# Attention scores as sixteen products on 32x32 tiles of the array

## The chip, the core and the metric

The kernel runs on one core of one Trainium2 chip. The metric is the device time of one execution in microseconds (us). Before the change it was 3142.55 us, the median of 3 runs (3142.08 to 3144.96).

## What is computed

Two attention layers on an image batch x of shape (4, 256, 64, 64), all in float32, with 8 heads of 32 channels. Cut to what matters here:

```python
# layer 0: keys and values at half resolution (1024 keys for 4096 queries)
q = einsum('oc,bchw->bohw', Wq, gn(x));  k, v = conv2x2(gn(x), Wk), conv2x2(gn(x), Wv)
attn = softmax((q.k + q.pos) * 32**-0.5);  x = x + v.attn
# layer 1: four areas of 1024 positions, each attends to itself
q, k, v = conv1x1(gn(x), w_qkv)
out = softmax(q.k * 32**-0.5).v + dwconv7(v, w_pe);  x = x + conv1x1(out, w_proj)
```

Both layers have the same attention: for each head, 4096 queries against 1024 keys, with a product over 32 channels for the scores and one over the keys for the result.

## The kernel before

The work is cut into units of 512 queries and 4 heads (16 units for an image and layer, 128 in all), and a unit into 8 key blocks of 128 keys. A key block of a unit is a "step"; there are 1024. The loop at the end of `direct_path` takes a step and a half in each of its 683 phases. In a phase, `scores(f)` computes one step over all 512 queries (`full`) and one half of another step, over 256 queries (`half`), for 4 heads each: eight products.

A score product (`score_product`, line 360) has the keys of one head as its weights, 32 rows (channels) by 128 columns (keys), and the head's queries as the moving operand, 32 rows by 512 or 256 columns. Head h lies in rows 32h to 32h+31 of the array, a "row group", so that the products of four heads run side by side in the four row groups. Each covers all 128 columns of the array, and writes 128 partitions of PSUM. The order of a phase is: `half` for heads 1 and 3, `full` for heads 0, 2, 1 and 3, a fence, and `half` for heads 0 and 2.

The three PSUM tiles of a phase (`a`, `b`, `c`, of two banks each, all called `s` in the profile) hold full heads 0 and 2, full heads 1 and 3, and the half step. In `c`, heads 0 and 1 share a bank, as heads 2 and 3 do. Two row groups may not write one bank at the same time, and so TensorE waits, at the fence, until the products of heads 1 and 3 have been counted in the semaphore `in_bank`. Each of these products adds one to it when it is done, and `bank_count` is the number that the fence waits for. What follows the fence in TensorE's queue is also behind it.

ScalarE takes the exponential of `a`, `b` and `c` (lines 401 and 412). In the next phase, `weighted` (line 426) multiplies these with the values: four products of 128 rows by 32 columns, one for each head, side by side in the four "column groups" of the array. VectorE adds up the exponentials (line 436) for the divisors. Between the scores and the `weighted` products of a phase, TensorE may have a side product (projections through `product`, line 164, the convolution on lines 973 and after, or the divisors, line 445), all of them four products of 32 columns side by side. A planner (`plan`, `task`, `side_parts`) chooses them by due times, before the program runs; the instruction order on each engine is written out by it.

Of the kernel before, what the change touches and what calls it, by code (L numbers as in the profile page):

```python
# [15 lines left out]
P = 128  # L16
# [3 lines left out]
NH, HD = 8, 32  # L20
# [39 lines left out]
def direct_path(  # L60
# [19 lines left out]
    V, S, G, T = nc.vector, nc.scalar, nc.gpsimd, nc.tensor  # L80
# [31 lines left out]
    first = [pool.tile([P, CT, CH], FP, tag="p", name=f"first_{c}", bufs=PB) for c in range(PB)]  # L112
    rest_of_first = pool.tile([P, 4, CH], FP, tag="acc", name="first", bufs=2)
    first += [rest_of_first[:, :2, :], rest_of_first[:, 2:, :]]
    for c in range(NCH):
# [27 lines left out]
        out=gmat, in_=gmat, compare_op=ALU.is_ge, fill=0.0, base=0,  # L143
# [3 lines left out]
        out=gmat, in_=gmat, compare_op=ALU.is_ge, fill=0.0, base=7,  # L147
# [18 lines left out]
    def ps_banks(n, name):  # L166
        return psum.tile([P, 2, CH], FP, tag=f"s{n}", name=name, bufs=1)
# [174 lines left out]
    in_bank, bank_count = tc.alloc_semaphore("in_bank"), [0]  # L342

    def acc_of(g):
        if g not in accs:
            accs[g] = pool.tile([P, 4, CH], FP, tag="acc", name="acc", bufs=2)
        return accs[g]

    def pair_of(h):
        return slice(2 * (h % 2), 2 * (h % 2) + 2)  # L350

    def acc_half(g, u):
        return acc_of(g).rearrange("p (l b) (u n) -> p u b l n", l=2, u=2)[:, u]

    def parts_of(f):

        full, half = (3 * f + 1) // 2, (3 * f // 2 + 1, 0) if f % 2 == 0 else (3 * f // 2, 1)
        return (full if full < last else None), (half if half[0] < last else None)

    def score_product(out, s, h, cols):  # L360
        g, j = divmod(s, NKT)
        rows, unit = slice(HD * h, HD * h + HD), units[g]
        return T.matmul(  # L363
            out, lhsT=unit[2]()[rows, unit[0], j * P : (j + 1) * P], rhs=unit[1]()[rows, cols], start=True, stop=True
        )

    def scores(f):

        full, half = parts_of(f)
        a, b, c = [ps_banks(n, "s") for n in ((0, 1, 2) if f % 2 == 0 else (0, 2, 1))]  # L370
        every = slice(0, CH)

        def half_product(h):

            u = half[1]
            return score_product(
                c[:, h // 2, HC * (h % 2) : HC * (h % 2) + HC], half[0], h, slice(HC * u, HC * u + HC)
            )

        if half is not None:  # L380
            for h in (1, 3):
                first = half_product(h).then_inc(in_bank, 1)
                tc.add_to_no_dep_group(f"first_{f}", first.ins)
                tc.no_tile_sem_insts.add(first.ins.name)
                bank_count[0] += 1
        for h in (0, 2, 1, 3):
            score_product((a, b)[h % 2][:, h // 2, :], full, h, every)
        if half is not None:
            fence = T.wait_ge(in_bank, bank_count[0])
            tc.declare_fence(fence.ins, group=f"first_{f}")  # L390
            for h in (0, 2):
                half_product(h)

        def exp_full(n):
            g, j = divmod(full, NKT)
            if j == 0:
                p = acc_of(g)[:, pair_of(n), :]
            else:
                p = pool.tile([P, 2, CH], FP, tag="p", name="p", bufs=PB)
            made_p[full, n] = p  # L400
            S.activation(p, (a, b)[n], AF.Exp, scale=SCALE)  # L401

        def exp_half():
            if half is None:
                return
            (g, j), u = divmod(half[0], NKT), half[1]
            if j == 0:
                p = acc_half(g, u)
            else:
                p = pool.tile([P, 2, CH], FP, tag="p", name="p", bufs=PB).rearrange("p b (l n) -> p b l n", l=2)  # L410
            made_p[half[0], 2 + u] = p
            S.activation(p, c.rearrange("p b (l n) -> p b l n", l=2), AF.Exp, scale=SCALE)  # L412

        return [lambda: exp_full(0), lambda: exp_full(1), exp_half]
# [663 lines left out]
    f = step = 0  # L1078
    before = []
    while f < PHASES or before or plan or side or quick or norms_left or to_add or to_divide:  # L1080
        now[0], phase[0] = step, f
        exps = scores(f) if f < PHASES else [lambda: None] * 3
        mine = []
        if f < PHASES:
# [641 lines left out]
```

## Time and profile before

| | us |
|---|---|
| median of 3 runs | 3142.55 |
| the profiled execution | 3136.07 |
| its span, first to last instruction | 3134.3 |
| TensorE (PE) matmuls, busy | 3059.4 (98%) |
| TensorE weight loads (PEld), busy | 1413.7 (45%) |
| VectorE (DVE) busy | 2516.0 (80%) |
| ScalarE (ACT) busy | 2456.4 (78%) |
| GpSimd (POOL) busy | 486.3 (16%) |

The granted clock of TensorE was 0.997 of full speed. The profiled execution is one run of the program under the hardware profiler. PE is the matmul, PEld the weight load that goes ahead of it. Matmuls are pipelined and the profiler models their ends, so a busy PE says that work is in flight, not that the array is full. A row of a group gives the line in the kernel, the engine and operation, the names of the tiles (output, then inputs), the shape, the count, then the busy time in us and the mean duration in ns, then the idle time of the engine ahead of them and what ended it. For a matmul, `32*128 32x512` is a weight block of 32 rows by 128 columns and a moving operand of 32 rows by 512 columns. A row of the timeline gives the start and length in us of a merged stretch of like instructions, and how many they are.

### The profile page before, as it was taken

The numbers are of one execution on the slowest core, as the hardware profiler recorded it, in microseconds if no ns is written. First come the engines' busy times: TensorE is split into PE (matmuls) and PEld (weight loads), VectorE is DVE, ScalarE is ACT, GpSimd is POOL, SyncE is SP. The second block draws the span as 40 slices with busy tenths as digits, with TensorE's granted clock in tenths as the row PEclk, the third lists the DMA queues.
The fourth block names the chain that finished last, engine by engine and source line by source line (L and its number), as shares of the span: only waits on it lengthen the run. The fifth ranks groups of instructions, "written<-read, shape, count | busy, mean of one in ns | idle before, by whom it ended". The sixth has DMA issues, their size and how long they took to land.

```text
span 3134.3 us, 87972 instructions
## 1 busy us (share of the span) xinstructions
PE 3059.4 (98%) x36218; PEld 1413.7 (45%) x36218; DVE 2516.0 (80%) x2719; ACT 2456.4 (78%) x2988; POOL 486.3 (16%) x923
## 2 busy tenths in 40 slices
PE   7999999999999999999999999999999999999997
PEld 4344444444455554444444444444444444444442
DVE  3788898878887777878778888788787888888887
ACT  2888878888788878878877777788887777778774
POOL 0111111111121111111111111111111111111111
PEclk9999999999999999999999999999999999999999
DMA  5243444556455646567777666664566556633212
GB/s 187 50 99 79 119 96 92 124 107 146 123 158 140 169 139 160 120 163 180 199 188 183 163 159 176 159 170 123 126 137 155 143 153 176 166 101 85 65 43 69
DMA packets 648236, 422.29 MB, mean 135 GB/s; under 512 B 411772, under 2 KB 556636, under 8 KB 647832
## 3 DMA queue, kind: packets, MB, share of 16 engines
q1 hardware_dynamic: 619384, 380.11, 47.7%
q0 software_dynamic: 28448, 36.48, 4.5%
q8 instruction: 292, 4.78, 0.7%
q14 instruction: 112, 0.92, 0.1%
HBM read 318.32 MB, written 98.09 MB: 133 GB/s over the span
## 4 chain that ended last, share of the span: by engine, by line
PE 46%; issue 4%; DMA 2%; ACT 1%; DVE 1%; POOL 1%; SPq 0%; ACTq 0%; DVEq 0%; POOLq 0%
PE s L363 16%; PE av L426 13%; PE q1ps L164 4%; PE ops L164 4%; PE k1ps L164 3%; PE conv_ps L973 2%; PE den L445 2%; PE vals_ps L164 1%; DMA recs<-few 1%; DVE acc L436 1%; ACT p L401 1%; POOL rb L474 0%; SPq L732 0%; DMA rb<-recs 0%; DMA cv<-conv 0%
## 5 line engine op out<-in xcount | busy, mean ns | idle before, releaser
L436 DVE TENSOR_TENSOR acc<-acc,p 128x1024 f32<-128x1024 f32 x1790 | 2113.2, 1218 | 457.9 <-ACT p L401 180.7
L401 ACT ACTIVATE p<-s 128x1024 f32<-128x1024 f32 x1194 | 1160.4, 1025 | 458.2 <-PE s L363 445.4
L412 ACT ACTIVATE p<-s 128x1024 f32<-128x1024 f32 x598 | 619.9, 1037 | 2.7 <-DVE acc L436 1.7
L363 PE MATMUL s<-q,k_A 32*128 32x256 f32 (+1 forms) x5464 | 559.8, 510 | 9.1 <-ACT p L401 6.2
L363 PE MATMUL s<-q,k_B 32*128 32x512 f32 (+1 forms) x5456 | 551.3, 509 | 2.6 <-ACT p L401 2.1
L363 PEld LDWEIGHTS s<-q,k_B 32*128 32x128 f32 x5456 | 342.8, 183 | 281.2 <-issue 55.1
L363 PEld LDWEIGHTS s<-q,k_A 32*128 32x128 f32 x5464 | 338.0, 183 | 291.7 <-ACT p L401 66.4
L426 PE MATMUL av<-p,v_A 128*32 128x256 f32 (+1 forms) x4784 | 454.0, 487 | 0.0
L426 PE MATMUL av<-p,v_B 128*32 128x512 f32 (+1 forms) x4776 | 451.2, 487 | 0.0
L474 POOL DMA_DIRECT2D rb<-recs x508 | 252.0, 502 | 510.0 <-DMA recs<-few 426.5
L472 POOL DMA_DIRECT2D recs<-few x127 | 70.1, 552 | 1413.5 <-DVE sums L471 1241.0
L426 PEld LDWEIGHTS av<-p,v_B 128*32 128x32 f32 x4776 | 148.5, 110 | 258.7 <-issue 233.1
L426 PEld LDWEIGHTS av<-p,v_A 128*32 128x32 f32 x4784 | 148.7, 110 | 235.6 <-issue 196.8
L401 ACT ACTIVATE acc<-s 128x1024 f32<-128x1024 f32 x172 | 166.9, 1023 | 78.7 <-PE s L363 78.5
L445 PE MATMUL den<-acc,ones 128*32 128x512 f32 x1024 | 144.6, 606 | 6.8 <-DVE acc L436 3.6
L464 POOL DMA_DIRECT2D few<-rows x127 | 72.3, 569 | 414.1 <-DMA rows<-den_sb 409.7
L164 PE MATMUL ops<-cv,wp_sb 128*32 128x512 f32 x1024 | 125.0, 602 | 5.2 <-DVE cv L744 4.4
L164 PE MATMUL k0ps<-taps,wkv 128*32 128x256 f32 x2048 | 124.9, 386 | 2.5 <-ACT taps L328 2.5
L164 PE MATMUL q1ps<-h,wqkv_sb 128*32 128x512 f32 x1024 | 123.8, 598 | 1.9 <-ACT q L701 1.9
L164 PE MATMUL vals_ps<-hv,wqkv_sb 128*32 128x512 f32 x1024 | 123.8, 598 | 0.2 <-ACT gmean_A L299 0.2
L164 PE MATMUL k1ps<-h,wqkv_sb 128*32 128x512 f32 x1024 | 123.5, 598 | 0.0
L164 PE MATMUL q0ps<-hq,wq_sb 128*32 128x512 f32 x1024 | 122.8, 597 | 0.0
(99 smaller groups left out, 2123.9 us busy)
## 6 DMA issues: line engine op xcount, KB each, us to landing
rows<-vals SPq DMA_DIRECT2D x384, 195.9 KB
rb<-recs POOLq DMA_DIRECT2D x508, 64.0 KB, 2.6
share<-vals SPq DMA_DIRECT2D x128, 195.9 KB
vala<-vout SPq DMA_DIRECT2D x128, 144.0 KB
vals<-vout SPq DMA_DIRECT2D x128, 144.0 KB
vc<-vala SPq DMA_DIRECT2D x64, 288.0 KB
band<-mats SPq DMA_DIRECT2D x96, 176.0 KB
hq<-in_x SPq DMA_DIRECT2D x32, 512.0 KB
```

The source lines that it names most:

```text
L164: T.matmul(out[cols, :], lhsT=lhsT[:, cols], rhs=rhs, start=start, stop=stop)
L363: return T.matmul(out, lhsT=unit[2]()[rows, unit[0], j * P : (j + 1) * P], rhs=unit[1]()[rows, cols], start=True, stop=True)
L401: S.activation(p, (a, b)[n], AF.Exp, scale=SCALE)
L412: S.activation(p, c.rearrange("p b (l n) -> p b l n", l=2), AF.Exp, scale=SCALE)
L426: T.matmul(out, lhsT=v[:, j, unit[0] * P + HD * h : unit[0] * P + HD * h + HD], rhs=rhs, start=(j == 0 and not u), stop=(j == NKT - 1), sk ...
L436: V.tensor_add(to, to, p)
L445: T.matmul(dens[g][HD * h : HD * h + HD, :], lhsT=ones, rhs=p(h), start=(n == 0), stop=(n == len(sets) - 1),)
L464: G.dma_start(few[:, 0, :], rows.rearrange("h (q n) -> (h q) n", n=CH // HD))
L472: G.dma_start(recs.rearrange("h (q n) -> (h q) n", n=CH // HD), few[:, 1, :])
L474: G.dma_start(rb[HD * h : HD * h + HD, :], recs[h : h + 1, :].to_broadcast([HD, CH]))
L973: T.matmul(ps[HD * m : HD * m + HD, (2 * k + i) * size : (2 * k + i + 1) * size].rearrange("p (y x) -> p y x", y=NY), lhsT=band[:, half].r ...
```

## The change

`score_product` issues four products where it issued one: the 128 keys are cut into four blocks of 32, and each block goes with its own 32 columns of weights to its own 32 partitions of the same output. The queries are the same for all four. Four heads give sixteen products on sixteen tiles of 32 rows by 32 columns. Because `score_product` now returns a list, the two half products in front of the fence become eight, each with its own increment of `in_bank`; the fence waits for eight more each phase instead of two. The order of everything else, on all engines, is as before, and no wait is added or taken away.

```diff
     def score_product(out, s, h, cols):
         g, j = divmod(s, NKT)
         rows, unit = slice(HD * h, HD * h + HD), units[g]
-        return T.matmul(
-            out, lhsT=unit[2]()[rows, unit[0], j * P : (j + 1) * P], rhs=unit[1]()[rows, cols], start=True, stop=True
-        )
+        return [
+            T.matmul(
+                out[n : n + HD], lhsT=unit[2]()[rows, unit[0], j * P + n : j * P + n + HD],
+                rhs=unit[1]()[rows, cols], start=True, stop=True,
+            )
+            for n in range(0, P, HD)
+        ]
...
         if half is not None:
             for h in (1, 3):
-                first = half_product(h).then_inc(in_bank, 1)
-                tc.add_to_no_dep_group(f"first_{f}", first.ins)
-                tc.no_tile_sem_insts.add(first.ins.name)
-                bank_count[0] += 1
+                for first in half_product(h):
+                    first.then_inc(in_bank, 1)
+                    tc.add_to_no_dep_group(f"first_{f}", first.ins)
+                    tc.no_tile_sem_insts.add(first.ins.name)
+                    bank_count[0] += 1
```

## The prediction

> **What bounds the kernel now.** I read the page's first section, then the groups with shapes kept apart, the groups of the score tile, a timeline of one phase, and last the trace's own records of single instructions and semaphore updates. The first view is the page:
>
> ```profile
> span 3134.3 us, 87972 instructions
> PE 3059.4 (98%) x36218; PEld 1413.7 (45%) x36218; DVE 2516.0 (80%) x2719; ACT 2456.4 (78%) x2988; POOL 486.3 (16%) x923
> ...
> q8 instruction: 292, 4.78, 0.7%
> ```
>
> (The last line is the queue that fetches instructions: packets, MB, share of the DMA engines.) TensorE has work in flight nearly always, at a granted clock of 0.997; VectorE and ScalarE have a fifth of the time to spare. So a change of TensorE's time per phase shows nearly one to one. There are 683 phases of 3134.3/683 = 4.59 us. The groups, with shapes kept apart:
>
> ```profile
> L363 PE MATMUL s<-q,k_A 32*128 32x512 f32 x2728 | 545.4, 616 | 0.4 <-ACT p L412 0.4
> ...
> L363 PE MATMUL s<-q,k_A 32*128 32x256 f32 x2736 | 451.5, 404 | 8.7 <-ACT p L401 6.2 <-ACT acc L401 1.8 <-ACT q L597 0.7
> ...
> L426 PE MATMUL av<-p,v_B 128*32 128x512 f32 x2392 | 313.0, 593 | 0.0
> ...
> L973 PE MATMUL conv_ps<-rows,band 88*32 88x128 f32 x3072 | 98.2, 276 | 0.2 <-DMA rows<-vals 0.2
> ```
>
> Each fp32 product is two matmuls ("passes"), each with a weight load. The score rows hold 10920 matmuls (5464 + 5456 on the page): 5460 products, eight a phase, four of 512 columns and four of 256 (682 phases have the halves). Next, the score tile's own view, and one phase in the timeline:
>
> ```profile
> L363 PEld LDWEIGHTS s<-q,k_A x5464: 181/184/186, 82.0 to 1597.8; 32*128 32x128 f32 x196
> L363 PE MATMUL s<-q,k_A x5464: 374/478/692, 82.0 to 1598.0; 32*128 32x256 f32 x147, 32*128 32x512 f32 x49
> ```
>
> ```profile
> 1507.82 0.61 PE L426 MATMUL av<-p,v_A 128*32 128x256 f32 x8
> ...
> 1508.36 1.19 PEld L363 LDWEIGHTS s<-q,k_A 32*128 32x128 f32 x16 [0.41 <-ACT vout L901]
> 1508.36 1.59 PE L363 MATMUL s<-q,k_A 32*128 32x256 f32 x16
> ...
> 1509.88 0.16 PEld L164 LDWEIGHTS vals_ps<-hv,wqkv_sb 128*32 128x32 f32 x8 [0.33 <-issue]
> 1509.88 0.64 PE L164 MATMUL vals_ps<-hv,wqkv_sb 128*32 128x512 f32 x4
> ```
>
> ```profile
> 1509.22 0.22 PEld L363 LDWEIGHTS s<-q,k_A 32*128 32x128 f32 x2
> ```
>
> The last line, a narrow window, is the first weight load behind the fence: 0.86 us after the phase's first. The single records, as medians over 679 phases and counted from the phase's first weight load, give this anatomy. Heads 1 and 3 (half) and 0 and 2 (full) start at 0.002 to 0.022 us, 6.7 ns apart. Their first pass lasts 104 ns more than the same shape later (692 against 587, 478 against 374): the exposed load of 128 weight columns. The halves' second pass starts at 0.322 and 0.328, the fulls' at 0.538 and 0.544; heads 1 and 3 (full) run from 0.548; heads 0 and 2 (half) start at 0.978 and 0.984, and the last column has streamed at 1.428. A 512-column pass occupies its tile 0.428 us (the starts of av's passes), a 256-column one 0.215, so a row group needs 2 x (0.428 + 0.215) = 1.286: streaming is the bulk of the 1.428. Before the scores there are 94 ns, after them 89 ns (medians), in which nothing streams.
>
> **The change, part by part.**
>
> *Streaming: nothing.* A 32x32 tile still takes a column of q at the same pace; sixteen tiles read as much per partition as av's four tiles of 128x32 do, and av gets its full pace (0.428 per pass, four at once). No row has 32x32 tiles.
>
> *Weight loads: about nothing.* A load of 32 columns exposed after a switch costs 25 ns (vals' first pass 617 against 592), so 79 ns less than now. But the first wave is now sixteen products, not four. Starts are 6.7 ns apart, which is four instructions, so the sixteenth tile starts at 0.027 + 15 x 0.0067 = 0.128. Today the fourth streams from 0.022 + 0.104 = 0.126. The gain is eaten by the queue.
>
> *The fence: the cost.* The fence on `in_bank` must see heads 1 and 3 done before heads 0 and 2 may write the same banks. Today two increments feed it, afterwards eight. The records put the two updates 42 to 43 ns apart in nearly every phase, though their matmuls start 6 ns apart, and no two of the 4338 updates by TensorE are closer than 42 ns. So I take eight at 42.5 ns. Today: the second passes start at 0.322 and end 0.374 later, the first update comes 0.014 after that (0.710), the second at 0.753, the weight load behind the fence at 0.858: 0.105 after the last update. That is just hidden: heads 0 and 2 are free at 0.97 and 0.98 and need 104 ns of weights. Afterwards:
> head 1's first tile streams from 0.027, its second pass starts at 0.242, the first update comes at 0.242 + 0.374 + 0.014 = 0.630, the eighth at 0.630 + 7 x 0.0425 = 0.928, the first load behind the fence at 1.033. Behind a fence the second product comes 35 ns later (the L973 products after one released at 1542.25 show 35 and then 7 ns each), so the eighth loads at 1.033 + 0.035 + 6 x 0.0067 = 1.108, streams from 1.133, and ends two passes of 0.215 later at 1.563. It could have started at 0.128 + 2 x 0.428 = 0.985. So the scores end 1.563 - 1.428 = 0.135 us later.
>
> What is queued behind: the two halves, then av or a side product, which need the array emptied of the scores' tile shape, so all of it moves by 0.135. ScalarE's third exp waits too, but it has about 1 us to spare in each phase. Some 5% of the phases already stall by 0.4 us or more on other things and may absorb it. Sum: 682 x 0.135 = 92 us, less 5% = 87 us. Against the profiled execution's 3136.07 us that is 3223; the median of the timed runs lies 6.5 us above that execution, so about 3230.
>
> Bounds. If updates of different tiles did not queue, the load behind the fence would come at 0.663 + 0.014 + 0.105 = 0.782, hidden, and the scores would end at 0.985 + 0.43 = 1.415: 682 x -0.013 = -9 us. The nearest row is the pair at 42.5, of different tiles too, so I take that.
>
> The Trainium skill ("TensorE: Matmul & The Clock Gate", The cost: per-tile semaphore tail) also says that increments of tiles serialize, at 26.3 ns each. By that figure the eighth update comes at 0.814, the end is at about 1.449, and the sum is an estimated +14 us; this trace's 42 ns differs, and the measurement decides.
>
> *Instructions.* 16380 more products are 32760 more matmuls and as many weight loads. In a phase the scores issue 128 instead of 32. The burst pace is 6.7 ns for four (214 ns for 128, hidden in 1.28 us of streaming). The longest dense stretch, L973's 64 matmuls with their loads, keeps 13.3 ns per instruction over 128, but streaming binds there, so that is an upper bound. At it, the 32 instructions behind the fence take 0.43 us and the eighth product starts some 0.32 later than above: another 682 x 0.32 = 220 us. I take the burst pace, as the row right behind a fence shows it, and keep the other for the range.
>
> The same page (Wait — 56ns, not 53.3ns?) says that matmul starts are never under 25 ns apart, which speaks against this change: 64 x 25 ns = 1.6 us would not fit the streaming, an estimated 0.32 us a phase or +218 us. This trace's starts on different tiles are 6.7 ns apart, so I do not use it.
>
> The instruction queue carries 65520 x 64 B = 4.2 MB more, some 256 packets of 1.2 us (0.7% of 16 engines' span over 292). The DMA engines are busy 0.77 of a dense stretch at 1500 us, so I cost this at nothing; were each packet waited for, it would be 307 us.
>
> **The rivals.**
>
> *Faster: no emptying between 32x32 and 128x32 tiles.* Both cut the columns in four. If the 94 and 89 ns vanished, 682 x 0.183 = 125 us would go, and with the fence's 92 the time would be about 3110. It decides once the switches shrink by more than 0.135 a phase. For it: products of one shape (vals to av) follow without a gap. Against it: rows still go from 128 to 32, and both directions show a gap today. 8%.
>
> *Hidden fence.* At half the measured spacing, 21 ns, the eighth update comes at 0.630 + 0.149 = 0.779, the load behind the fence at 0.884, the eighth product at 0.98, in time: 3142.55 - 9 = 3133. A few ns more of spacing gives up to 3160. Against it, 42 ns in every phase. 13%.
>
> *Slow issue.* The queue does not hold the 32 instructions behind the fence, or the sixteen tiles of a wave start late: up to 92 + 220, so 3265 to 3455. Nothing in the trace shows more than 16 in a burst. 18%.
>
> *The tiles of a row wait for each other.* A product's second pass stands ahead of the next product in program order. Today the next one overtakes it, but it is always in another row group, or for av in another column group. If tiles sharing a row group queued in order, each product would start a pass after the one before: 4 x 0.643 + 0.43 = 3.0 us against 1.43, +1.57 x 682 = 1070 us, about 4210. 7%. That the change does nothing at all is not open: the instructions are there.
>
> **How the numbers follow.** Forecast 3230 with 54% (3190 to 3265), and the rivals as above. The range 3133 to 3440 takes in the forecast, the hidden fence and nearly all of slow issue, and leaves out the no-emptying and row-queue cases, some 18% with the edges. Within 0.2% (about what a measurement of this kernel can tell from no change) lie 3136 to 3149: 8%, from the hidden fence. Faster: 8% and a few points of the hidden fence, 12%. Slower: 80%.
>
> **What would show it.** Right: x68978 matmuls; eight updates of `in_bank` 42 ns apart; the first weight load behind the fence at about 1.03 us instead of 0.86 while heads 0 and 2 stand idle; first passes 25 ns over the later ones; switches still of 90 ns. Wrong: a load behind the fence before 0.95; starts of sixteen tiles spread over more than 0.15 us; tiles of one row starting 0.2 us apart; a gap that is gone at a switch.

## The result, and the profile after

The changed kernel takes 3378.51 us (median of 4 runs, 3367.82 to 3385.28) against 3142.32 us before (4 runs, 3141.22 to 3144.96): a ratio of 1.0749, with a 95% interval of 1.0735 to 1.0764. The forecast was +88 us, the measured difference is +236 us. The sign was right, and the size was off by a factor of 2.7.

The page's first section, and its row of the queue that fetches instructions:

```profile
span 3366.0 us, 153492 instructions
PE 3299.6 (98%) x68978; PEld 1498.6 (45%) x68978; DVE 2522.3 (75%) x2719; ACT 2467.0 (73%) x2988; POOL 484.6 (14%) x923
...
q8 instruction: 548, 8.98, 1.1%
```

The products are there (68978 matmuls). VectorE and ScalarE do the same work in the same time, and PE is again 98% busy. That share says only that some tile has work in flight. What is lost in this kernel is lost while PE counts as busy. The instruction queue has its 256 more packets. The granted clock was 0.998.

The groups, with shapes kept apart (busy time in us, mean ns of one):

```profile
L364 PE MATMUL s<-q,k_A 32*32 32x512 f32 x10912 | 657.1, 599 | 0.1
L364 PE MATMUL s<-q,k_A 32*32 32x256 f32 x10944 | 496.4, 385 | 6.5 <-issue 2.4 <-ACT p L406 2.0 <-ACT acc L406 1.3
```

There are four times as many matmuls, and each one is shorter than before (599 ns against 616, 385 against 404), because less of a weight load is exposed in front of a first pass. So no single product became slower. The time lies between products. The timeline of one phase (start, length, how many), and, of the weight loads alone, a narrow window in it:

```profile
1505.34 0.61 PE L431 MATMUL av<-acc,v_A 128*32 128x256 f32 x8
1505.89 1.97 PE L364 MATMUL s<-q,k_A 32*32 32x256 f32 x64
1507.78 1.06 PE L450 MATMUL den<-acc,ones 128*32 128x512 f32 x8
```

```profile
1506.56 0.10 PEld L364 LDWEIGHTS s<-q,k_A 32*32 32x32 f32 x1
```

The stretch of score matmuls is 1.97 us long; it was 1.59. The narrow window holds one load, 0.67 us after the phase's first (1505.884). It is not the load behind the fence, but one that the prediction had not put on the path: the second product of full head 1. The same phase cut into stages, for the score tile alone (stage, length, then busy time and count of PE and of PEld, ScalarE, granted clock, DMA share, GB/s), shows its place:

```profile
1505.88:1506.01 0.13, 0.12 (x16) 0.13 (x30) 0.00 (x0) 1.00 1.10 216
1506.01:1506.34 0.33, 0.33 (x24) 0.22 (x29) 0.00 (x0) 1.00 0.99 195
1506.34:1506.55 0.21, 0.21 (x25) 0.10 (x1) 0.00 (x0) 1.00 0.46 104
1506.55:1506.83 0.28, 0.28 (x25) 0.27 (x13) 0.00 (x0) 1.00 0.39 103
```

In the first 0.13 us sixteen products start. In the third row, 0.46 to 0.67 us, one load is made, although the eight tiles of heads 1 and 3 come free between 0.46 and 0.50. Then thirteen loads come in 0.28 us.

The trace's single records (medians over 679 phases, in us from the phase's first score weight load) give the whole order:

| event | before | after |
|---|---|---|
| the first wave starts | 0.002 to 0.022 (4) | 0.002 to 0.120 (16) |
| second pass of heads 1 and 3 (half) | 0.322, 0.328 | 0.242 to 0.288 |
| updates of `in_bank` | 0.710, 0.753 | 0.629, then 42.5 ns apart, to 0.927 |
| full heads 1 and 3: first product starts | 0.548 | 0.458 |
| their others load | (0.555 starts) | 0.674, then 42.5 ns apart; the last starts at 0.932 |
| first and second load behind the fence | 0.858, 0.893 | 1.032, 1.127 |
| halves 0 and 2 end | 1.428 | 1.681 |
| full heads 1 and 3 end | 1.40 | 1.810 |
| gaps in front of and behind the scores | 94, 89 ns | 94, 89 ns |

The last row but two was the end of the scores before, and the last row but one is the end after. The means from trace to time: a phase's score stretch went from 1.472 to 1.831 us (+0.359, less than the median's +0.382), and the mean gaps around it gave back 0.021. The sum, 0.339 x 682 = 231 us, is the difference of the two spans (3366.0 - 3134.3 = 231.7).

The full heads 1 and 3 run late for a reason that the prediction had not asked about. Seven of their eight products load 44 ns or so after one update of `in_bank` each (0.629 and 0.674, and so on at the same pace), although nothing in the kernel makes them wait for that semaphore. This gave the theories that the experiments were to tell apart. In program order a phase has 32 products: 1 to 8 are the halves of heads 1 and 3, 9 to 16 full heads 0 and 2, 17 to 24 full heads 1 and 3, and 25 to 32, behind the fence, the halves of heads 0 and 2.

**Theory W (window).** TensorE holds 64 instructions, which are 16 products of four instructions each (load, matmul, load, matmul). They go out in program order, each when it is complete and its increment is written; only then does a new one come in. The 16 products of the first wave fill it. The 17th (full head 1's first) gets in piece by piece as the first leaves: its load at 0.243, its first pass at 0.458. The 18th waits until the first product of half head 1 is out: 0.242 + 0.374 = 0.616, and its increment at 0.629. The next products get in as the others of heads 1 and 3 leave, and since each of these carries an increment, they leave 42.5 ns apart. The last, head 3's fourth, starts at 0.932, has its second pass at 1.383 and ends 0.428 later: 1.811 (measured 1.810). In the same way the 26th, the second product behind the fence, waits for the 9th, full head 0's first: 0.508 + 0.587 = 1.095 (its load is at 1.127).

**Rivals.** The increments alone make the delay, and without them the 18th product would start when its tile is free, at about 0.5; or TensorE is short of instructions, and the new ones come at a slow pace wherever they stand.

### The profile page after: what moved, and what is told of

The parts are those of the page before. It is cut to its first block, busy times and chain, and to the rows that moved or that the text cites. A ratio compares the mean times of both kernels' runs of the same rounds, so it can differ in the third digit from the quotient of the medians.

```text
span 3366.0 us, 153492 instructions
## 1 busy us (share of the span) xinstructions
PE 3299.6 (98%) x68978; PEld 1498.6 (45%) x68978; DVE 2522.3 (75%) x2719; ACT 2467.0 (73%) x2988; POOL 484.6 (14%) x923
## 5 line engine op out<-in xcount | busy, mean ns | idle before, releaser
L364 PE MATMUL s<-q,k_A 32*32 32x512 f32 (+1 forms) x21856 | 680.0, 492 | 6.5 <-issue 2.4
L364 PE MATMUL s<-q,k_B 32*32 32x512 f32 (+1 forms) x21824 | 675.0, 492 | 0.9 <-issue 0.4
L364 PEld LDWEIGHTS s<-q,k_A 32*32 32x32 f32 x21856 | 377.0, 103 | 310.3 <-ACT p L417 78.8
L364 PEld LDWEIGHTS s<-q,k_B 32*32 32x32 f32 x21824 | 380.0, 103 | 301.7 <-issue 69.4
```

Of the source, the lines that this page charges most:

```text
L364: T.matmul(out[n : n + HD], lhsT=unit[2]()[rows, unit[0], j * P + n : j * P + n + HD], rhs=unit[1]()[rows, cols], start=True, stop=True,)
```

## The experiments

**Two increments in sixteen tiles.** Only the last column block of heads 1 and 3 counts; the sixteen products stay.

```diff
-                for first in half_product(h):
-                    first.then_inc(in_bank, 1)
+                for n, first in enumerate(half_product(h)):
+                    if n == P // HD - 1:
+                        first.then_inc(in_bank, 1)
+                        bank_count[0] += 1
...
-                    bank_count[0] += 1
```

> The changed kernel, but only the last column block of heads 1 and 3 counts into in_bank: two increments a phase instead of eight. Theory W (TensorE holds 64 instructions at once and lets them go in program order, each when its matmul is complete and its increment is written; a product is four instructions, so product k of a phase gets in when product k-17 is out): the increments no longer add 42 ns each, but the second wave (full heads 1 and 3) still waits until the first product is complete at 0.62 us, and the halves of heads 0 and 2 until full head 0 is complete at 1.10. The scores end at 1.68 us in the phase instead of 1.81: 3378.5 - 682 x 0.13 = about 3290. Rival I (the increments alone hold things up): the fence is hidden and the scores end at 1.41 to 1.43: 3133 to 3145. Rival S (TensorE's instructions are supplied too slowly for four times as many): hardly changed, 3340 to 3380.

Measured: 3308.13 us (4 runs), ratio to before 1.0535 (1.0518 to 1.0553). The phase ends at 1.682. Updates come at 0.680 and 0.773, and the first load behind the fence at 0.878. The stages of a phase that starts at 1504.677, columns as above:

```profile
1504.68:1504.81 0.13, 0.13 (x16) 0.13 (x31) 0.00 (x0) 1.00 0.78 167
1504.81:1505.14 0.33, 0.33 (x25) 0.22 (x28) 0.00 (x0) 1.00 0.71 183
1505.14:1505.31 0.17, 0.17 (x25) 0.10 (x1) 0.00 (x0) 1.00 0.74 235
1505.31:1505.48 0.17, 0.17 (x29) 0.15 (x14) 0.00 (x0) 1.00 0.67 188
```

The same hole stands in the third row: one load between 0.46 and 0.63, with only two increments in the phase and none at that place. It ends at 0.65, when the first half product is complete (0.616). After it the fourth row has fourteen loads in 0.17 us, 16.7 ns a product in the records, and not 42.5. So the hole is not the increments' doing; the pace after it is. The end at 1.682 is that of the halves 0 and 2 in the changed kernel (1.681): the 26th product's place, not the fence. Measured against the same kernel before, the increments make about 70 us of the 236 (3378.5 - 3308.1), and what is left with two increments, 5.35% of 3142, is 168 us. Theory W had expected 3290: the median end moved by the 0.13 us that it named, but the mean stretch of scores shrank by 0.108 us only, or 74 us in 682 phases.

**One increment.** As with two increments, but with a narrower condition: only the last block of head 3 counts.

```diff
+                    if h == 3 and n == P // HD - 1:
```

> The changed kernel (four blocks of 32), where only the last block of head 3 counts into in_bank: one increment a phase. Theory W: what ends the phase is the entry of the halves of heads 0 and 2, which waits for full head 0 to be complete at 1.10 us, not the increments: the scores end at 1.68 us as with two increments, 3300 to 3310. Rival I (increments alone): less than with two, by up to 682 x 0.04 = 29 us, about 3280.

Measured: 3312.74 us (one run), the update at 0.747, the end at 1.681. The fence opens earlier still and nothing comes of it: in sixteen tiles, once the increments are two, the fence no longer counts. (The time is just above the 3300 to 3310 that W gave.)

**Full heads 0 and 2 first, in sixteen tiles.** By W what the 18th product waits for is the product first in program order. So the order is turned, and nothing else.

```diff
+        for h in (0, 2):
+            score_product((a, b)[h % 2][:, h // 2, :], full, h, every)
         if half is not None:
             for h in (1, 3):
...
-        for h in (0, 2, 1, 3):
+        for h in (1, 3):
```

> The changed kernel with the order of the first wave turned: full heads 0 and 2, then half heads 1 and 3 (with their eight increments), full heads 1 and 3, fence, half heads 0 and 2. Same instructions. Theory W: what leaves first is now a long product, complete at 1.04 us instead of 0.62, so full heads 1 and 3 get in at 1.09 to 1.19, and the increments are written only after full head 2 is out, at 1.13 to 1.43: the scores end at 2.07 to 2.12 us instead of 1.81, about 3570. Rivals I and S (no going out in order): the tiles are free at the same times as before, within 0.05 us a phase, 3370 to 3415.

Measured: 3582.35 us (one run), the phase ends at 2.152. The weight loads of a phase that starts at 1504.356, in the timeline (the brackets give the idle time before):

```profile
1504.36 0.40 PEld L364 LDWEIGHTS s<-q,k_A 32*32 32x32 f32 x33 [0.84 <-ACT vout L908]
1505.00 0.10 PEld L364 LDWEIGHTS s<-q,k_A 32*32 32x32 f32 x1 [0.24 <-issue]
1505.43 0.23 PEld L364 LDWEIGHTS s<-q,k_A 32*32 32x32 f32 x14 [0.33 <-issue]
1505.97 0.21 PEld L364 LDWEIGHTS s<-q,k_A 32*32 32x32 f32 x16 [0.31 <-issue]
```

33 loads come in one stretch (16 products, and the first of the 17th), then one for its second pass, and fourteen, the other seven products of heads 1 and 3, only at 1.07, when a full product of head 0 is complete. Their tiles had been free since 0.51 to 0.57. The last sixteen are behind the fence. A slow pace of issue has no reason to hold them until 1.07; W has. It had put their starts at 1.09 to 1.19 and the end at 2.07 to 2.12; they start at 1.078 to 1.178, and the end comes later than it said because the updates do (1.216 to 1.513 against 1.13 to 1.43).

The 17th product, the one that got in, shows that places are not given to whole products. Its first load comes at 0.297, when the first product is far from complete (1.042). Its first pass starts at 0.640, 26 ns after the first product's first pass ends (0.614), although its tile is free at 0.510.

**The same turn in the kernel before.** There a phase has eight products, 32 instructions, so no window of 64 can bind. What it shows is the order in which increments are written.

> The kernel before with the same turn of order (full heads 0 and 2, half heads 1 and 3, full heads 1 and 3, fence, half heads 0 and 2); its phase has 32 instructions, which always fit in 64. Theory W: only the going out in order acts: the two increments are written after full head 2 is complete (1.13 us), at 1.18 and 1.23 instead of 0.71 and 0.75, the fence opens at 1.33, the scores end at 1.90 instead of 1.43: 3142 + 682 x 0.47 = about 3460. If increments are written as each matmul ends, whatever stands before it: 3137 to 3150.

Measured: 3409.58 us (one run), the end at 1.913. The weight loads of a phase that starts at 1513.528:

```profile
1513.53 0.74 PEld L363 LDWEIGHTS s<-q,k_A 32*128 32x128 f32 x12 [0.41 <-ACT p L414]
1514.87 0.33 PEld L363 LDWEIGHTS s<-q,k_A 32*128 32x128 f32 x4 [0.60 <-issue]
```

All twelve loads ahead of the fence come in one stretch, with no hole, and the four behind it only at 1.34 (0.858 in the order as it was). The halves' second passes start at 0.335 and 0.342 and have ended by 0.72, but the updates come at 1.196 and 1.238: after the full products that now stand ahead of them (0.542 + 0.587 = 1.129). A finished product does not report until those before it in program order are complete. That is the second half of W, shown without the window. The phase lost 0.485 us, 331 us in 682 phases, and the time rose by 271: other stalls shrank, and the means of stretch and gaps give +0.421, 287 us. The expectation's 3460 left that out.

**Two column blocks, 64 columns each.** Eight products fill a wave, and the phase has 16, which are 64 instructions. By W none waits for a place; the updates are four.

```diff
-                out[n : n + HD], lhsT=unit[2]()[rows, unit[0], j * P + n : j * P + n + HD],
+                out[n : n + 2 * HD], lhsT=unit[2]()[rows, unit[0], j * P + n : j * P + n + 2 * HD],
...
-            for n in range(0, P, HD)
+            for n in range(0, P, 2 * HD)
```

> Two products of 64 columns for each head instead of four of 32: eight tiles, four increments a phase. Theory W: the first wave is eight products, 32 instructions, and everything up to the last half is within 64, so nothing waits to get in; the exposed weight load is about 0.05 us instead of 0.10; four increments from 0.66 to 0.78, the first load behind the fence at 0.89, the end at 1.42 to 1.45: 3135 to 3155. Rival I: the same, since four increments are 0.13 us instead of 0.30. Rival S (supply of instructions): 64 instead of 128 and 32, a third of the cost, 3142 + 79 = about 3220.

Measured: 3135.26 us (10 runs), ratio 0.9992 (0.9982 to 1.0001); end 1.420. In the timeline of a phase:

```profile
1510.37 0.64 PEld L364 LDWEIGHTS s<-q,k_A 32*64 32x64 f32 x24 [0.84 <-ACT cout L989]
1511.26 0.23 PEld L364 LDWEIGHTS s<-q,k_A 32*64 32x64 f32 x8 [0.25 <-issue]
```

All 24 loads ahead of the fence come in one stretch, with no hole, and the eight behind it at 0.89. Twice the products cost nothing; four times cost 236 us. A cost per instruction would have shown a third of it here, some 79 us.

**Two column blocks and two increments.** With no window in the way the fence is what is left on the path. The edit is that of two blocks, and of the blocks of heads 1 and 3 only the last counts:

```diff
+                    if n == P // HD // 2 - 1:
```

> Two products of 64 columns for each head, and only the last of each of heads 1 and 3 counts into in_bank: two increments a phase. Theory W (64 instructions, out in program order): the last increment is written at 0.66 + 0.04 to 0.06 instead of 0.78, the first load behind the fence comes at about 0.82 instead of 0.89, which is in time for heads 0 and 2 (free at 0.91 to 0.93), and the scores end at 1.365 to 1.39 instead of 1.42: 3135 - 682 x 0.03 to 0.05 = 3100 to 3115. If the increments do not matter at four: 3130 to 3140.

Measured: 3125.38 us (6 runs), ratio 0.9941 (0.9928 to 0.9954): 0.6% less than the kernel before, and less than the changed one. The updates come at 0.673 and 0.733, and the loads of the halves at 0.84:

```profile
1506.88 0.64 PEld L364 LDWEIGHTS s<-q,k_A 32*64 32x64 f32 x24 [0.41 <-issue]
1507.72 0.25 PEld L364 LDWEIGHTS s<-q,k_A 32*64 32x64 f32 x8 [0.20 <-issue]
```

The phase ends at 1.386, 0.042 before the kernel before, or 28 us over 682 phases; about 18 us reach the time, less than was expected (3100 to 3115).

**One increment in the kernel before.** Only head 3 counts.

```diff
+                if h == 3:
+                    first.then_inc(in_bank, 1)
+                    bank_count[0] += 1
```

> The kernel before, where only head 3 counts into in_bank: one increment a phase instead of two. Under theory W head 1 is out before head 3, so that one count stands for both. The increment comes at 0.715 instead of 0.753, the first load behind the fence at 0.82 instead of 0.858, and its 0.104 us of weights are there when heads 0 and 2 are free (0.97, 0.98): the scores end at 1.41 instead of 1.428: 3138 - 682 x 0.015 = about 3128, range 3122 to 3138.

Measured: 3134.58 us (8 runs), ratio 0.9975 (0.9964 to 0.9987). One update at 0.727 in place of the second at 0.753, the load behind the fence at 0.832, the end at 1.413. The end gains 15 ns and no more, because the next limit stands there: heads 0 and 2 start at 0.978 and 0.984 as before, when their tiles are free.

The fence gains 26 ns here, not 42, and the other runs show why. Updates are 42.5 ns apart where every product counts, 59.5 where every second does (two blocks, two increments), and 93 where every fourth does (two increments). So a product takes 16.7 ns to go out, and an increment adds about 26. The same two prices give the late update in the turned kernel before. The first product ends at 1.122, two more take 0.033, full head 2 carries an increment of its own for another wait (0.026), and a written update shows 0.014 after its product is out: 1.195, measured 1.196.

**Two shapes in a phase.** To see which products of which heads the window holds, heads 1 and 3 had 64 columns and heads 0 and 2 had 32.

```diff
+        rows, unit, wide = slice(HD * h, HD * h + HD), units[g], (2 if h % 2 else 1) * HD
...
-            for n in range(0, P, HD)
+            for n in range(0, P, wide)
```

> The changed kernel, but heads 1 and 3 are cut in two products of 64 columns and heads 0 and 2 stay cut in four of 32: 24 products a phase, 12 of them in the first wave, and four increments. Theory W (a product gets in when the one 17 places ahead is out): full heads 1 and 3 are products 13 to 16 and get in at once, so their part is as in two_blocks; of the halves of heads 0 and 2 (17 to 24), the last three must wait for the first three products of full head 0 (complete at 1.07 us) and start at 1.10 to 1.14, so that the scores end at 1.59 us, and the time is 3230 to 3250. No such window: 1.42 us, 3135 to 3145. If tiles of 64 and of 32 columns cannot run side by side, the row groups take turns: at least 0.6 us more a phase, over 3550.

Measured: 4239.97 us (one run). The experiment did not answer its question. Weight loads in the timeline:

```profile
1500.14 0.21 PEld L364 LDWEIGHTS s<-q,k_A 32*64 32x64 f32 x8 [0.84 <-ACT taps L328]
1500.73 0.18 PEld L364 LDWEIGHTS s<-q,k_A 32*32 32x32 f32 x16 [0.39 <-issue]
1501.74 0.21 PEld L364 LDWEIGHTS s<-q,k_A 32*64 32x64 f32 x8 [0.84 <-issue]
1502.76 0.18 PEld L364 LDWEIGHTS s<-q,k_A 32*32 32x32 f32 x16 [0.81 <-issue]
```

The two shapes take turns: each set of loads waits until the set of the other shape has run. The phase ends at 3.13, because row groups that would run side by side now stand one behind the other. So the places of W were not tested this way.

## Why the prediction was wrong in size

*Streaming: nothing.* Right. Later passes of 512 columns last 587 ns in both kernels.

*Weight loads: about nothing.* Right where it was worked out: first passes are 22 to 25 ns over later ones (609 to 612 against 587), the sixteenth product starts at 0.120 where 0.128 was expected, and the halves' second pass starts at 0.242 as written. What the step stopped short of is the wave after that one.

*The fence.* Right to the ns as far as it went: first update 0.629 (0.630), eighth 0.927 (0.928), the load behind it 1.032 (1.033). Its end was wrong: 1.681 for the halves, not 1.563, since the second product behind the fence waits for a place until 1.127 and the rest follow at 16.7 ns a product, not 6.7. The 42.5 ns between updates held. But it is not the price of an increment alone, as the prediction read it when it set the 26.3 ns aside: about 26 of it is the increment, and 16.7 the product's own going out.

*Instructions: the step that failed.* The prediction weighed more instructions only as a pace, so much time for each, and asked of the queue only whether it holds the 32 behind the fence. It let full heads 1 and 3 start as soon as their tiles are free. The runs show places: products 18 to 24 wait until products 1 to 7 have left, and these leave 42.5 ns apart, as each carries an increment. The end that sets the phase is theirs, 1.810, a chain that the prediction does not have. Of the 236 us, about 168 are there with two increments, and about 70 come with the other six. The 87 us of the fence are not in addition to this; with the window full, six increments less save 1.810 - 1.682 = 0.128 us a phase, which happens to be close to the 0.135 that was priced for another path.

*The rivals.* "Slow issue" gave a time that holds the result (3265 to 3455) under a name that comes near, "the queue does not hold the 32 instructions", but its price was a pace of 13.3 ns an instruction. The pace is 16.7 ns for a product's four, 4.2 each, once there is a place. "No emptying" is refuted by the gaps, 94 and 89 ns as before; "hidden fence" by updates 42.5 ns apart; "tiles of a row wait for each other" by sixteen starts in 0.12 us. The 25 ns between starts that the prediction quotes and sets aside would have given +218 us, near the result, and for the wrong reason: starts are as close as before.

*The instruction queue's cost of nothing.* Nothing speaks against it: 548 packets, and in the kernel of two blocks, with its own added instructions, the time did not rise.

The Trainium skill ("TensorE: Matmul & The Clock Gate", The mechanism) gives TensorE a reorder window that is 64 deep, and this was there to be held against 128 instructions a phase. The runs agree with the 64: 33 loads and no more before the first wait in the turned order, no hole with 16 products, a hole with 32. That the 17th product gets in one load and one pass at a time (0.297, 0.640) speaks against 16 whole products. As every matmul here has its load, the runs can't tell 64 instructions from 32 matmuls. The same section says that matmuls start and end in program order. Ends, as far as increments show them, do (1.196 and 1.238 in the turned kernel before). Starts don't: products of other tiles start ahead of second passes that stand before them (the sixteenth product at 0.120, the first one's second pass at 0.242), and the measurement decides.

The Trainium skill ("TensorEngine Tiling (Array Packing)", Key Properties) says that a change of tiling mode drains TensorE. The gaps of 94 and 89 ns agree with that, and the kernel of two shapes shows what it costs when it comes inside a phase: 4240 us.

What stays open: whether the loads hold places of their own, and why about 10 of the 28 us that the path lost in the kernel of two blocks and two increments did not reach the time. (In its trace the phases that take longer than the median one cost 61 us in all, 48 before; what holds them is not shown.)

## What to carry to other kernels

Where one product is cut into many for more tiles, first count the instructions in a wave against the places that TensorE has, and then ask which product must be complete, in program order, before the next wave gets in; that wait does not depend on whether its tile is free. Put the short products first, and let only the last product of a group report, since each report holds up all that stands behind it by about 26 ns, on top of the 16.7 that a product takes to go out. A cut into as many pieces as fit at once may cost nothing where the next finer one costs 7%, and a busy share of 98% shows neither.

## What the runs showed of the hardware that was not expected

- An increment is not written when its product is done, but when all products before it in program order are complete: 1.196 us instead of about 0.72.
- An increment costs about 26 ns, on top of the 16.7 ns that each product takes to go out: updates are 42.5, 59.5 and 93 ns apart with one, two and four products to an update.
- Products get into a full queue 16.7 ns apart (four instructions), where four idle row groups start theirs 6.7 ns apart.
- An exposed fp32 weight load costs 22 to 25 ns for 32 columns, 52 ns for 64 (639 against 587) and about 104 for 128.
- Tiles of 32 by 64 and of 32 by 32 never ran side by side: a phase of both took 3.13 us, one of either alone 1.42 or 1.81.
